# A conditional block of attention-free layers on one core: the hand-over tables of the second half in another order of the same steps

## The chip, the cores and the metric

The kernel runs on one core of one Trainium2 chip. Five engines work side by side, each through its own instructions in program order: TensorE (PE; its weight loads are listed as PEld), VectorE (DVE), ScalarE (ACT), GpSimd (POOL) and SyncE (SP), which only issues transfers. They wait for one another through semaphores. The metric is the device time of one execution in microseconds (us), as the median over several runs.

## What is computed

The input is 32 batches of 128 tokens of 512 numbers. The block has two halves. The first changes masked tokens only, the second all of them:

```
m = mask[:, :, None]
shift, scale, gate_msa = split(silu(t) @ ada_w + ada_b, 3)
norm = where(m, layernorm(x) * (1 + scale) + shift, 0)
ssm_out = where(m, fwd(norm) + bwd(norm), 0)        # two MLPs of 512 x 512 x 512, gelu
x = x + gate_msa * ssm_out
shift_mlp, scale_mlp, gate_mlp = split(silu(t) @ ffada_w + ffada_b, 3)
ff_norm = layernorm(x) * (1 + scale_mlp) + shift_mlp
h = gelu(ff_norm @ ff_w1 + ff_b1)                   # 512 -> 1024
return x + gate_mlp * (h @ ff_w2 + ff_b2)           # 1024 -> 512
```

All of it is float32.

## The kernel before

**The first half.** The masked tokens are packed into slots, 128 to a tile, and only these pass through the first half. Its results are written to rows in DRAM (`x1_rows`).

**The second half** does the feed-forward part for the 32 batches in four pairs p = 0 to 3 of two sides with four batches each. A side's x is loaded by SyncE (`load_side`; the steps X0 and X1 load the sides of pair p + 2 at the end of pair p). Then `take_first_half` (L904) writes the first half's results over the masked rows: per tile of 128 tokens one indirect transfer on GpSimd's queue, called a gather here. The steps x20 to x27 are the eight gathers for pair 2; a step name that begins with "n" belongs to the next pair (nx20 stands in the table of pair 0 and x26 and x27 in that of pair 1). A gather needs its tile's load to have landed. VectorE then takes the statistics of each tile (steps b00 to b13, L937 and L938; v0, v1 at L942; r0, r1 on GpSimd at L945), and the tile is normalised (n..), turned (z..), moved across partitions by SyncE (m...) and scaled by ScalarE (c..., L968).

**Both matrix products are done by a fast scheme with seven products per 2 x 2 split, on two levels.** In the first product (`FirstProduct`) the outer products are the streams 1, 2, 5, 6, 3, 7, 4, and each has seven inner groups P1 to P7, of four matmuls each (L1155). So 6P3 is a group on PE, the third inner product of stream 6. Around the groups of a stream j stand its sums: jc5 (ScalarE, a copy out of PSUM), js (VectorE L1175, seeds one bank from the other), jw12 and jw22 (GpSimd L1182), jk11 and others (ScalarE L1197), je (VectorE L1188), jj22 and jj21 (VectorE L1207), ja.. (GpSimd L1216). All VectorE sums among these read a PSUM bank (`a_m` in the rows). Stream sums of tokens (steps tj0 to tj3, lines 1091, 1095, 1098 and 1101 for j = 1 to 4; blocks A1 to A4 at L1021) read and write SBUF alone. Those of pair p + 1 are named nt10 to nt43 in the table of pair p.

In the second product (`SecondProduct`) a group is PnU0 and the like (L1387, up to eight matmuls), F.., B., T., U. are VectorE sums (F02 at L1294), and three of its products are split again (`Inner`): 5i3, 6i4, 7i4 and so on are groups of eight small matmuls on PE (L1473), S1i4 to S4i4 their sums on GpSimd (L1462), C5i4 copies on ScalarE (L1500), V6i4 and V7i4 sums on VectorE (L1505), J40 a sum on VectorE (L1420). The result is multiplied by the gate and added to x: K... on ScalarE (L1343), G... on GpSimd (L1349) or VectorE (L1331), R... (L1356, L1338), and stored by SyncE (o.., L1369).

**What sets the order.** Each of these steps is put into a table by name, and `ORDER[p]` is a text of names. The steps are run in the order of the text, so each engine's program is the text's order as far as its own steps go:

```
class Steps:
    def put(self, name, f, *args):
        assert name not in self.todo, name
        self.todo[name] = lambda: f(*args)

    def run(self, order):
        for name in order or list(self.todo):
            self.todo.pop(name)()
        assert not self.todo, list(self.todo)
...
        steps.run(ORDER.get(p, "").split())
```

No scheduler stands behind it: what an engine's queue holds at its head, it waits for, and everything behind waits with it. The table of pair p runs from stream 6 of that pair (6P1 is its first name in pair 0) to stream 2 of the next pair (n2P4 is near its end). The gather is this:

```
    def take_first_half(p, xs, which=range(2 * G)):
        for i in which:
            b = 2 * p * G + i
            nc.gpsimd.indirect_dma_start(
                out=xs[i // G][i % G // 2][:, i % 2],
                ...
```

At the end of pair p six gathers of pair p + 2's tiles stand on GpSimd, and behind them the first GpSimd sum of the next pair's stream 6, 6w12, which 6e on VectorE and then 6P3 on PE wait for.

## Time and profile before

| what | value |
|---|---|
| three runs of the kernel before | 451.76, 452.56, 452.85 us; median 452.56 |
| the profiled execution | 454.02 us, its span 452.3 us |
| granted TensorE clock, mean | 0.994 |
| busy in the span | PE 436.5, DVE 336.8, POOL 263.9, ACT 204.8 us |
| moved by DMA | 70.89 MB, mean 157 GB/s |
| the reordered part of the span | from 99.11 us to the end |

A row of the trace in time shows start, duration, engine, line, operation, the names of output and inputs, shape, and in brackets how long the engine sat idle before it and what released it. "x4" says that four instructions which follow one another are joined in one row. TensorE's ends are modelled, so its rows overlap by some tenths of a microsecond, and the spacing of starts tells more. All numbers are microseconds from the start of the span. The profile describes one execution, so its span and its own time belong together, and the median of the runs is a little lower.

### The profile page before, as it was taken

What the parts mean: (1) busy time and instruction counts of PE and PEld (TensorE: products, weight loads), DVE (VectorE), ACT (ScalarE), POOL (GpSimd) and SP (SyncE); (2) the same over time, 40 slices, a digit from 0 to 9 for tenths busy, and PEclk for the clock granted to TensorE, in tenths of its full rate; (3) what the DMA queues carried; (4) which work ended last, traced back from release to release, by engine and by line L of the source; (5) the groups of instructions that cost most, each with busy time, mean ns of one, the idle gap of its engine ahead of it and who ended that gap; (6) DMA issues with size and microseconds to landing.
All of it is one profiled execution on the core that took longest, in us unless ns stands there. A gap on an engine that the chain in (4) does not pass through costs nothing.

```text
span 452.3 us, 7030 instructions
## 1 busy us (share of the span) xinstructions
PE 436.5 (97%) x2435; PEld 372.1 (82%) x2435; DVE 336.8 (74%) x592; ACT 204.8 (45%) x453; POOL 263.9 (58%) x226
## 2 busy tenths in 40 slices
PE   8999989999999999989999989999999999999992
PEld 4884675688888998878889978888899988888992
DVE  5788788878996689969762799898727994454265
ACT  3133127254582773534856635438756244553120
POOL 4211460089942894998618666896187616922991
PEclk9999999999999999999999999999999999999997
DMA  7999449894155507851375068614750354113005
GB/s 252 367 395 410 168 89 326 274 349 137 36 145 94 135 1 243 279 159 43 95 139 140 2 223 269 188 40 77 154 145 1 144 205 124 39 57 131 0 5 186
DMA packets 57044, 70.89 MB, mean 157 GB/s; under 512 B 34740, under 2 KB 36108, under 8 KB 55982
## 3 DMA queue, kind: packets, MB, share of 16 engines
q1 hardware_dynamic: 51742, 67.72, 47.7%
q0 software_dynamic: 3008, 2.15, 1.7%
q10 hardware_dynamic: 2256, 0.54, 0.7%
q8 instruction: 21, 0.34, 0.3%
q14 instruction: 17, 0.14, 0.1%
HBM read 56.71 MB, written 13.70 MB: 156 GB/s over the span
## 4 chain that ended last, share of the span: by engine, by line
PE 72%; DMA 11%; DVE 6%; POOL 5%; issue 5%; ACT 0%; POOLq 0%; SPq 0%; DVEq 0%; ACTq 0%
PE a_m L1155 17%; PE e_m L1155 13%; PE e_o L1387 12%; PE a_o L1387 11%; PE one_P L1473 6%; DMA fw<-in_L_cond_ff_w_dram 3%; PE po_s L222 3%; DMA w<-in_L_cond_bwd_w_dram 3%; PE a_o L1473 3%; PE five_P L1473 2%; PE e_o L1473 2%; DMA x_wide<-t_s 2%; POOL x L904 2%; POOL t L1349 1%; DMA x<-in_x_dram 1%
## 5 line engine op out<-in xcount | busy, mean ns | idle before, releaser
L1349 POOL TENSOR_TENSOR t<-t,gate 128x512 f32<-128x512 f32 x16 | 24.0, 1507 | 62.5 <-ACT t L1343 62.5
L1182 POOL TENSOR_TENSOR ha<-p_m,ha 128x512 f32<-128x512 f32 x20 | 25.5, 1274 | 48.2 <-ACT ha L1197 36.8
L968 ACT ACTIVATE xT<-xT,modT 128x128 f32<-128x128 f32 x112 | 46.4, 485 | 4.7 <-DMA xT<-xn 3.3
L904 POOL DMA_INDIRECT x<-x_rows,slot_i x24 | 31.5, 1311 | 8.2 <-issue 6.6
L1207 DVE TENSOR_TENSOR hb<-a_m,hb 128x512 f32<-128x512 f32 x40 | 27.2, 679 | 10.0 <-PE a_m L1155 7.3
L1197 ACT COPY ha<-e_m 128x512 f32<-128x512 f32 x32 | 18.6, 586 | 35.0 <-PE e_m L1155 29.2
L1125 ACT ACTIVATE hb<-hb,biasT 128x256 f32<-128x256 f32 x64 | 28.2, 500 | 13.0 <-DVE hb L1207 13.0
L1387 PE MATMUL a_o<-t,s 128*128 128x256 f32 x128 | 29.6, 379 | 0.0
L1387 PE MATMUL a_o<-fw,ha 128*128 128x256 f32 x128 | 29.4, 379 | 0.0
L1387 PE MATMUL e_o<-fw,s 128*128 128x256 f32 x128 | 29.2, 380 | 0.1
L1125 ACT ACTIVATE ha<-e_m,biasT 128x256 f32<-128x256 f32 x48 | 20.1, 469 | 19.9 <-PE e_m L1155 19.9
L1387 PE MATMUL e_o<-fw,ha 128*128 128x256 f32 x128 | 28.4, 379 | 0.0
L222 PE MATMUL po_s<-w,h_s 128*128 128x512 f32 x64 | 28.4, 594 | 0.0
L1387 PEld LDWEIGHTS e_o<-fw,s 128*128 128x128 f32 x128 | 24.2, 190 | 3.8 <-DVE s L1294 0.5
L1182 POOL TENSOR_TENSOR hb<-p_m,hb 128x512 f32<-128x512 f32 x20 | 26.3, 1319 | 1.4 <-DVE hb L1207 1.0
L1387 PEld LDWEIGHTS a_o<-fw,ha 128*128 128x128 f32 x128 | 24.3, 190 | 3.3
L1387 PEld LDWEIGHTS e_o<-fw,ha 128*128 128x128 f32 x128 | 24.3, 190 | 3.3
L1387 PEld LDWEIGHTS a_o<-t,s 128*128 128x128 f32 x128 | 23.7, 190 | 2.9
L1398 DVE TENSOR_TENSOR e_o<-a_o,p_o 128x512 f32<-128x512 f32 x16 | 11.1, 693 | 18.1 <-PE a_o L1387 17.1
L1155 PE MATMUL a_m<-xT,tw 128*128 128x256 f32 x96 | 24.3, 379 | 0.0
L1169 ACT COPY p_m<-e_m 128x512 f32<-128x512 f32 x27 | 15.7, 585 | 17.6 <-PE e_m L1155 17.6
L1155 PE MATMUL e_m<-s,fw 128*128 128x256 f32 x92 | 23.7, 381 | 0.0
(280 smaller groups left out, 1150.8 us busy)
## 6 DMA issues: line engine op xcount, KB each, us to landing
x<-in_x_dram SPq DMA_DIRECT2D x16, 512.0 KB, 7.1
tw<-t_rows SPq DMA_DIRECT2D x16, 512.0 KB, 3.6
gate<-gate_rows SPq DMA_DIRECT2D x8, 1024.0 KB
out_dram<-x SPq DMA_DIRECT2D x15, 512.0 KB, 4.2
xT<-xn SPq DMA_DIRECT2D x104, 64.0 KB, 2.2
tw<-t_rows SPq DMA_DIRECT2D x16, 384.0 KB
ada_f<-in_L_cond_ffada_w_dram SPq DMA_DIRECT2D x4, 768.0 KB, 14.7
ada_a<-in_L_cond_ada_w_dram SPq DMA_DIRECT2D x4, 512.0 KB, 3.5
```

The source lines that it names most:

```text
L222: nc.tensor.matmul(po, h[f][:, ts(i, P)], w[:, f, :], start=(f == 0 and seeded is None), stop=(f == HC - 1), skip_group_check=seeded is no ...
L904: nc.gpsimd.indirect_dma_start(out=xs[i // G][i % G // 2][:, i % 2], out_offset=None, in_=x1_rows, in_offset=bass.IndirectOffsetOnAxis(ap= ...
L968: nc.scalar.activation(out, src, AF.Identity, bias=shift, scale=scale)
L1125: nc.scalar.activation(dst[:, n], src[:, n], AF.Gelu_apprx_tanh, bias=biasT[:, f : f + 1])
L1155: nc.tensor.matmul(bank[:, ts(n, QT)].rearrange("p (i b c) -> p i b c", i=2, c=R), self.w_block(j, product)[:, ts(n, P)], self.x_block(j, ...
L1169: nc.scalar.copy(self.p5[j], self.fives[j].rearrange("p (n s) -> p n s", n=2))
L1182: nc.gpsimd.tensor_tensor(self.place(RESULT[j], c), self.p5[j], other, ALU.add)
L1197: nc.scalar.copy(self.place(RESULT[j], c), src)
L1207: nc.vector.tensor_tensor(dst, a, other, ALU.add)
L1349: nc.gpsimd.tensor_tensor(view, view, self.gate[side][:, 2 * c : 2 * c + 2, part], ALU.mult)
L1387: nc.tensor.matmul(bank[:, ts(i, D // 2)], src[:, k, ts(i, P)], w[:, k, :], start=False, stop=True, skip_group_check=True,)
L1473: nc.tensor.matmul(out[:, i % out.shape[1]], src[:, k, ts(i, P)], w[:, k, :], start=(start and (i == 0 or out.shape[1] == 1) and k == 0), ...
```

## The change

The texts of `ORDER` for all four pairs (lines 1695 to 1774) are replaced. No step is added or removed, no line elsewhere differs, and the engines execute as many instructions as before. A line or two of the table of pair 0, around the end, shows the kind of the difference:

```
-            nt20 o01 nt30 o10 n1P4 nt12 X0 n5P1 n5s nt33 n2P3 n2k12 nx20 n2P7 n1k21 n5P2 nt32 n5P6
+            n2k11 n2w12 n2e nt32 n2w22 nx20 n5c5 nt22 n5P1 n5s n2P7 nt20 nx21 n2P3 nx23 n5P2 nt13
```

What happens to the places that matter here is read from the engines' programs.

**The end of pair 0 on VectorE.** From the sum n2e (the row of `e_m_2`) on. L1091 to L1101 are token sums of pair 1, `hb<-a_m_2` at L1207 is n2j22 the first time and n2j21 the second, and `e_m_5` at L1188 is n5e. Before:

```order
L1188 TENSOR_TENSOR e_m_2_1570<-a_m_2_1571,ha_1564 128x512
L1095 TENSOR_TENSOR xn_sy_1607<-sx_1442,s_1_1443 128x512
L1098 TENSOR_TENSOR s_1_1443<-s_1_1443 128x2x256
L1091 TENSOR_TENSOR sx_1442<-xT_1_1280 128x512
L1098 TENSOR_TENSOR s_1_1444<-s_1_1444 128x256
L1098 TENSOR_TENSOR xT_1_1280<-xT_1_1280 128x2x256
L1207 TENSOR_TENSOR hb_1565<-a_m_2_1571,hb_1565 128x2x256
L1101 TENSOR_TENSOR s_1_1443<-s_1_1443,xn_sy_1607 128x2x256
L1095 TENSOR_TENSOR xn_sy_1607<-sx_1442,xT_1_1280 128x512
L1095 TENSOR_TENSOR xn_sy_1607<-sx_1442,xT_0_1234 128x512
L1101 TENSOR_TENSOR s_1_1444<-s_1_1444,xn_sy_1607 128x256
L1207 TENSOR_TENSOR hb_1565<-a_m_2_1571,hb_1565 128x2x256
```

Now:

```order
L1188 TENSOR_TENSOR e_m_2_1572<-a_m_2_1573,ha_1569 128x512
L1098 TENSOR_TENSOR xT_1_1298<-xT_1_1298 128x2x256
L1095 TENSOR_TENSOR xn_sy_1632<-sx_1464,xT_1_1298 128x512
L1095 TENSOR_TENSOR xn_sy_1632<-sx_1464,s_1_1465 128x512
L1091 TENSOR_TENSOR sx_1464<-s_1_1466 128x256
L1207 TENSOR_TENSOR hb_1570<-a_m_2_1573,hb_1570 128x2x256
L1095 TENSOR_TENSOR xn_sy_1632<-sx_1464,xT_0_1203 128x512
L1101 TENSOR_TENSOR xT_1_1298<-xT_1_1298,xn_sy_1632 128x2x256
L1101 TENSOR_TENSOR xT_0_1203<-xT_0_1203,xn_sy_1632 128x2x256
L1098 TENSOR_TENSOR s_1_1465<-s_1_1465 128x2x256
L1188 TENSOR_TENSOR e_m_5_1615<-a_m_5_1616,p_m_5_1630 128x512
L1207 TENSOR_TENSOR hb_1570<-a_m_2_1573,hb_1570 128x2x256
```

Five token sums (one of them 256 wide) stood between n2e and n2j22; now four do (one 256 wide). Four more led to n2j21; now four lead to n5e, and n2j21 follows it at once.

**The inner products of pair 1 on GpSimd.** `si_1_P` and `hb` at L1462 are the sums S1i4 to S4i4 (the last one, `hb<-hb,si_1_P`, is S4i4, which 7i4 reads), and L1349 are gate products (G001 of the tile `t_001`, G101 of `t_101`). Before:

```order
L1462 TENSOR_TENSOR si_1_P_2116<-hb_1565 128x512
L1349 TENSOR_TENSOR t_100_2005<-t_100_2005,gate_0_1906 128x512
L1462 TENSOR_TENSOR si_1_P_2163<-si_1_P_2116,hb_1565 128x512
L1462 TENSOR_TENSOR hb_1565<-hb_1565 128x2x256
L1349 TENSOR_TENSOR t_101_2175<-t_101_2175,gate_0_1906 128x512
L1349 TENSOR_TENSOR t_001_2113<-t_001_2113,gate_0_1906 128x512
L1462 TENSOR_TENSOR hb_1565<-hb_1565,si_1_P_2163 128x2x256
```

Now:

```order
L1462 TENSOR_TENSOR si_1_P_2136<-hb_1570 128x512
L1462 TENSOR_TENSOR si_1_P_2138<-si_1_P_2136,hb_1570 128x512
L1349 TENSOR_TENSOR t_001_2120<-t_001_2120,gate_0_1867 128x512
L1462 TENSOR_TENSOR hb_1570<-hb_1570 128x2x256
L1462 TENSOR_TENSOR hb_1570<-hb_1570,si_1_P_2138 128x2x256
L1349 TENSOR_TENSOR t_101_2164<-t_101_2164,gate_0_1867 128x512
```

Two gate products stood directly ahead of S4i4, and now one stands ahead of S3i4 and the other behind S4i4.

**The end of pair 1 on VectorE**, with the same steps of the next pair; `e_m_2` at L1188 is n2e again. Before:

```order
L1188 TENSOR_TENSOR e_m_2_2219<-a_m_2_2220,ha_2229 128x512
L1095 TENSOR_TENSOR xn_sy_2255<-sx_2157,s_2_2134 128x256
L1095 TENSOR_TENSOR xn_sy_2255<-sx_2157,s_2_2133 128x512
L1098 TENSOR_TENSOR xT_0_1860<-xT_0_1860 128x2x256
L1098 TENSOR_TENSOR xT_1_1943<-xT_1_1943 128x2x256
L1098 TENSOR_TENSOR s_2_2133<-s_2_2133 128x2x256
L1207 TENSOR_TENSOR hb_2230<-a_m_2_2220,hb_2230 128x2x256
L1095 TENSOR_TENSOR xn_sy_2255<-sx_2157,xT_0_1860 128x512
L1098 TENSOR_TENSOR s_2_2134<-s_2_2134 128x256
L1101 TENSOR_TENSOR s_2_2133<-s_2_2133,xn_sy_2255 128x2x256
L1101 TENSOR_TENSOR s_2_2134<-s_2_2134,xn_sy_2255 128x256
L1207 TENSOR_TENSOR hb_2230<-a_m_2_2220,hb_2230 128x2x256
```

Now:

```order
L1188 TENSOR_TENSOR e_m_2_2228<-a_m_2_2229,ha_2234 128x512
L1098 TENSOR_TENSOR s_2_2177<-s_2_2177 128x2x256
L1091 TENSOR_TENSOR sx_2237<-s_2_2178 128x256
L1098 TENSOR_TENSOR xT_1_1943<-xT_1_1943 128x2x256
L1095 TENSOR_TENSOR xn_sy_2256<-sx_2237,s_2_2178 128x256
L1098 TENSOR_TENSOR s_2_2178<-s_2_2178 128x256
L1207 TENSOR_TENSOR hb_2235<-a_m_2_2229,hb_2235 128x2x256
L1095 TENSOR_TENSOR xn_sy_2256<-sx_2237,xT_0_1888 128x512
L1098 TENSOR_TENSOR xT_0_1888<-xT_0_1888 128x2x256
L1101 TENSOR_TENSOR s_2_2177<-s_2_2177,xn_sy_2256 128x2x256
L1188 TENSOR_TENSOR e_m_5_2246<-a_m_5_2247,p_m_5_2266 128x512
L1101 TENSOR_TENSOR s_2_2178<-s_2_2178,xn_sy_2256 128x256
```

n2j22 is the seventh row in both; ahead of it stood one narrow token sum (256 wide) and four wide ones, and now three narrow and two wide stand there; three token sums further on comes n5e, where four led to n2j21 and n5e stood behind the last row shown.

Other places are told in words. On PE the groups of pair 0 read 6i4, 4i7, n1P5, n1P1, 2i4, 7i4 where 6i4, n1P5, 7i4 stood; in pair 1 they read 6i4, n1P5, 7i4, n1P1 where 6i4, n1P5, n1P1, 7i4 stood. In pair 2 the VectorE sum F02 stands ahead of the statistics b11, b12 and b13, where it stood behind them and v1. In pair 1 the statistics b12 stand ahead of 4s and behind x26 and x27, where they stood behind 3j21.

142 lines of the change are left out of this document (71 added, 71 removed).

## The prediction

> **What bounds the kernel now.** I first read the page's table of busy time. It names the engine that is never idle for long:
>
> ```profile
> PE 436.5 (97%) x2435; PEld 372.1 (82%) x2435; DVE 336.8 (74%) x592; ACT 204.8 (45%) x453; POOL 263.9 (58%) x226
> ```
>
> TensorE (PE) is busy for 436.5 of the span's 452.3 us. The change removes no matmul, so all it can gain is PE's idle time, 15.8 us. The second view is the table by stage; its columns are start:end, length, then busy time of PE, PEld, DVE, ACT and POOL, the granted clock, the DMA share and GB/s:
>
> ```profile
> 0.00:99.11 99.11, 95.93 (x540) 64.91 (x541) 78.08 (x190) 33.39 (x72) 32.49 (x51) 1.00 0.84 295
> 99.11:168.00 68.89, 68.89 (x383) 62.35 (x382) 58.19 (x93) 40.20 (x91) 50.13 (x39) 1.00 0.40 98
> 312.00:443.30 131.30, 131.30 (x772) 120.06 (x770) 78.63 (x114) 59.87 (x135) 77.69 (x61) 1.00 0.32 95
> 443.30:452.30 9.00, 0.27 (x3) 0.08 (x1) 3.44 (x8) 0.00 (x0) 0.00 (x0) 0.71 0.52 179
> ```
>
> The reordered part runs from 99.11 on. Up to there PE is idle for 3.18 us, and nothing the change moves lies there. The last row is the tail behind the last matmuls: 8.73 us idle, and the last steps stand as they did. That leaves 15.8 − 3.2 − 8.7 = 3.9 us of idle, none of it in the 200 us of the second and third row. The third view, PE's own rows in time (start, duration of the group, matmuls, what it waited for), shows the four places where it lies:
>
> ```profile
> 168.72 1.13 PE L1155 MATMUL e_m<-s,fw 128*128 128x256 f32 x4
> 170.24 1.16 PE L1473 MATMUL one_P<-fw,hb 128*128 128x128 f32 x8 [0.40 <-DVE xn_d L1505]
> ...
> 195.50 1.03 PE L1155 MATMUL a_m<-sx,tw 128*128 128x256 f32 x4
> 198.45 1.13 PE L1155 MATMUL e_m<-xn_sy,tw 128*128 128x256 f32 x4 [1.92 <-DVE e_m L1188]
> 199.42 1.03 PE L1155 MATMUL a_m<-xn_sy,tw 128*128 128x256 f32 x4
> ...
> 261.24 1.03 PE L1155 MATMUL a_m<-xT,fw 128*128 128x256 f32 x4
> 263.72 1.13 PE L1473 MATMUL one_P<-fw,hb 128*128 128x128 f32 x8 [1.46 <-POOL hb L1462]
> ...
> 308.81 2.26 PE L1387 MATMUL e_o<-fw,s 128*128 128x256 f32 x8
> 310.91 1.03 PE L1155 MATMUL a_m<-xT,tw 128*128 128x256 f32 x4
> 311.77 1.03 PE L1155 MATMUL e_m<-s,tw 128*128 128x256 f32 x4
> ```
>
> I measure a loss from start to start, since the ends are modelled. A group of four takes 311.77 − 310.91 = 0.86, one of eight 1.72, and a group that had to wait costs 0.1 more itself (198.45 to 199.42 is 0.97). So the losses are A, at 168.72: 1.52 − 0.86 + 0.1 = 0.76. B, at 195.50: 2.95 − 0.86 + 0.1 = 2.19. C, at 261.24: 2.48 − 0.86 + 0.1 = 1.72. D, at 308.81: 2.10 − 1.72 = 0.38. Together 5.05 us (more than the 3.9 of idle, since a group's modelled end, 1.03 behind its start, reaches past the 0.86): the most that any order of these steps can win.
>
> **Why B is late.** B is the group 6P3 of pair 1, and it waits for a VectorE sum (6e), which waits for the GpSimd sum 6w12, which stands behind six gathers. GpSimd's rows (start, duration), the first three of the gathers, two of the others, and 6w12:
>
> ```profile
> 183.93 3.50 POOL L904 DMA_INDIRECT x<-x_rows,slot_i  x1 [0.28 <-POOL hb L1182]
> 187.73 2.35 POOL L904 DMA_INDIRECT x<-x_rows,slot_i  x1 [0.30 <-issue]
> 190.38 2.08 POOL L904 DMA_INDIRECT x<-x_rows,slot_i  x1 [0.30 <-issue]
> 192.77 0.99 POOL L904 DMA_INDIRECT x<-x_rows,slot_i  x1 [0.30 <-issue]
> 195.37 1.00 POOL L904 DMA_INDIRECT x<-x_rows,slot_i  x1 [0.30 <-issue]
> 196.39 1.27 POOL L1182 TENSOR_TENSOR ha<-p_m,ha 128x512 f32<-128x512 f32 x1
> ```
>
> From 6w12's start to PE's is 198.45 − 196.39 = 2.06. A gather takes 1.00 and 0.30 to the next, but three took 3.50, 2.35 and 2.08. VectorE beside them:
>
> ```profile
> 185.76 0.69 DVE L1098 TENSOR_TENSOR xT<-xT 128x512 f32<-128x512 f32 x1
> 186.36 0.69 DVE L1207 TENSOR_TENSOR hb<-a_m,hb 128x512 f32<-128x512 f32 x1
> 189.10 0.69 DVE L1207 TENSOR_TENSOR hb<-a_m,hb 128x512 f32<-128x512 f32 x1
> 191.50 0.70 DVE L1175 TENSOR_TENSOR e_m<-a_m,ha 128x512 f32<-128x512 f32 x1
> ```
>
> The first gather ends at 187.43, 1.07 after the sum of L1207 starts; the second at 190.08, 0.98 after the next; the third at 192.46, 0.96 after L1175. These three read a PSUM bank (a_m). What fills the time between them, without a gap, are token sums of lines 1091 to 1101, both of whose inputs lie in SBUF, each 0.60 behind the last (186.36 − 185.76; 0.34 where it is 256 wide). I take from this: a gather that stands before an unbroken row of such sums is served when the row is broken by a sum that reads PSUM, and ends about 1.05 after. The next boundary supports it and tempers it:
>
> ```profile
> 276.66 2.39 POOL L904 DMA_INDIRECT x<-x_rows,slot_i  x1 [1.39 <-DMA x<-in_x_dram]
> 279.35 1.15 POOL L904 DMA_INDIRECT x<-x_rows,slot_i  x1 [0.30 <-issue]
> 286.13 1.28 POOL L1182 TENSOR_TENSOR ha<-p_m,ha 128x512 f32<-128x512 f32 x1
> ...
> 278.00 0.69 DVE L1207 TENSOR_TENSOR hb<-a_m,hb 128x512 f32<-128x512 f32 x1
> ```
>
> The gather of 2.39 ends 1.05 after the L1207 sum at 278.00; the one at 279.35 passed between two token sums. Here 6w12 came at 286.13 and PE lost nothing: 6P3 ran in its slot (288.95), 0.76 after 286.13 + 2.06.
>
> **The change, part by part.** Nothing is added or removed; four orders are replaced. Every step has the same instructions, its DMAs included, so what moves is what waits for what.
>
> *A.* 7i4 waited for the VectorE step V6i4. In the new order 4i7, two first groups of the next pair and 2i4 stand between 6i4 and 7i4, over 3 us of PE work: the wait is gone. +0.76.
>
> *C.* 7i4 of pair 1 waited for the GpSimd step S4i4 (L1462), which stood behind two gate products:
>
> ```profile
> 258.88 3.56 POOL L1349 TENSOR_TENSOR t<-t,gate 128x512 f32<-128x512 f32 x2 [4.06 <-ACT t L1343]
> 262.40 1.26 POOL L1462 TENSOR_TENSOR hb<-hb,si_P 128x512 f32<-128x512 f32 x1
> ...
> 253.36 2.54 DVE L1021 TENSOR_TENSOR s<-xT 128x1024 f32<-128x1024 f32 x1
> ```
>
> GpSimd had idled 4.06 for ScalarE's K011 before. Now one product stands ahead of S3i4 and S4i4 and the one that needs K011 behind them, which frees 4.06 + 1.78; 7i4 itself stands one group, 0.86, earlier. What is late next is VectorE: V6i4 now stands directly behind A1 (L1021) and a few 0.6 us sums. A1 has lasted 2.54 (the row at 253.36) where others last 1.2; with 1.2 the cover holds, with 2.54 some 0.3 is lost. I take half, 0.15: +1.57.
>
> *D.* P5U0 of pair 2 waited for F02:
>
> ```profile
> 309.20 0.68 DVE L1294 TENSOR_TENSOR s<-hb 128x512 f32<-128x512 f32 x1
> ```
>
> It stood behind two tiles' statistics; it now stands ahead of them. They are 1.6 of VectorE work and the wait was 0.38: gone. +0.38.
>
> *B.* The order of both engines at the end of pair 0 is new. Let R be the slot in which 6P3 would start without loss; 6w12 has to start by R − 2.06. PE reaches n2P6, which releases n2e, 18 groups ahead: R − 15.5; with the product's own time and the sum's wait n2e starts at R − 13.8. It and three wide token sums and a narrow one (4 × 0.60 + 0.34) lie ahead of n2j22, a PSUM sum: R − 11.0. That and four wide ones lie ahead of n5e (R − 8.0), n5e itself, n2j21, two wide and two narrow ones ahead of 6s (R − 5.2). The first gather is ready at about R − 13: it writes rows into a tile that the load X0 fills, which follows a store, and before it landed at 183.15, 13.2 ahead of the slot 195.50 + 0.86 = 196.36:
>
> ```profile
> 177.09 6.06 DMA x<-in_x_dram
> ```
>
> So by the rule the first ends 1.05 after n2j22 (R − 10.0), the second after n5e (R − 7.0; n2j21 begins too early for the third), the third after 6s (R − 4.1), and the last three at 1.30 each: R − 0.2. 6w12 starts there and 6P3 at R + 1.9. Loss 1.9 for 2.19: +0.29. From below, gathers that all pass between sums as the one at 279.35 did make it 0; from above, with the first opening missed for a later X0, one gather more is left at 1.30: 3.2. I keep 1.9, the value that the three openings before B gave.
>
> *E, new.* At the end of pair 1 n2j22 now comes after two wide and three narrow token sums, and n5e three wide ones later. Counted in the same way from n2P6, 17 groups ahead: n2j22 at R − 10.5, n5e at R − 8.1, and n2j21, which waits for its product, lets the third through; the others end at R − 9.4, − 7.0, − 5.7, − 3.7, − 2.4 and − 1.1. 6w12 starts at R − 1.1, 6P3 at R + 1.0: lost 1.0, where before nothing was. From below 0, from above 2.3 (one opening missed, 1.30 more): −1.0.
>
> The sum: 0.76 + 1.57 + 0.38 + 0.29 − 1.0 = 2.0 us. The profiled execution took 454.02, 1.7 more than its span; less 2.0 it is 452.0. The median of the three runs shown is 452.56, so 2.0 less there is 450.6. All losses gone: 452.56 − 5.05 = 447.5. B at 3.2, E at 2.3 and the waits A, C and D replaced by others of 1.5 in all: 7.0 lost for 5.05, 454.5.
>
> **The rivals.** *First: a gather waits for one sum at most.* Then it costs 1.00 and half a sum, 0.35; six with their 0.30 are 9.6, from R − 13 to R − 3.4, ahead of R − 2.06 at both ends of a pair, and B and E are 0: 5.05 − 0.15 = 4.9 gained, 447.7. The gather at 279.35 (1.15) speaks for it. The one of 3.50 speaks against it: several sums started and ended inside it. [...]
>
> *Second: the new orders miss the openings.* B costs 3.2 and E 2.3 while A, C and D are won: 5.05 − 5.5 − 0.15 = 0.6 lost, 453.2. For it: both places rest on a load that lands after a store, and the trace shows one gather already waiting 1.39 for that load.
>
> *Third: VectorE stands behind a landing.* Its queue is in program order, and b12, the statistics of a gathered tile, now stands ahead of 4s in pair 1, with x26, its gather, shortly before; before, it stood behind 3j21:
>
> ```profile
> 209.42 1.01 POOL L904 DMA_INDIRECT x<-x_rows,slot_i  x1 [0.30 <-issue]
> 213.60 0.68 DVE L937 BATCH_NORM_STATS2 st<-x 128x6 f32<-128x512 f32 x1
> ...
> DMA to landing us min/median/max: 2.6/3.8/7.6
> ```
>
> Behind b12 wait 4s and 3j21, and PE's 4P2 waits for 4s. Between x26 and 4P2 lie some six groups, 5.4; a landing of 2.7, b12's 0.7 and 4s's 0.7 leave 1.3. From a landing of 4.0 on it costs; at the longest, 7.6, 3.6: 450.6 + 3.6 = 454.2, slower. For it: half of the landings are over 3.8. Against it: the long ones are counted with the time in which the gather itself was held, and none of those is held at this place, where no token sums run.
>
> **How the numbers follow.** The forecast's case, 450.6, has 0.50: its rule explains four gathers of five, its sizes are counted. The first rival has 0.24, for the one gather that slipped. The second has 0.15, the third 0.11. A measurement here tells 0.3% (1.36 us) from no change. The forecast's case lies 0.6 inside that border (451.2); I give two thirds of it, 0.34, to faster, 0.14 to the same and 0.02 to slower. With the first rival's 0.24 and 0.01 of the second, faster has 0.59; the second's other 0.14 brings the same to 0.28; the third brings slower to 0.13. The range from 447.5 to 453.9 takes in the first two rivals and leaves out the third. The forecast's case alone, with B between 0.6 and 3.2 and E between 0 and 2.3, has 448.3 to 453.2.
>
> **What would show it.** In the changed profile, PE shows no wait between 6i4 and 7i4 in pair 0, at most 0.3 in pair 1, and none before P5U0; 6w12 of pairs 1 and 2 still starts directly behind the sixth gather, and the two first gathers of each last over 2 us and end about 1.05 after n2j22 and n5e. I am wrong if those gathers take 1.0 to 1.7 (then the first rival), if PE's rows show a wait behind b12 (the third), or if PE's idle from 99.11 to the tail differs from 3 us by over 1.5.

## The result, and the profile after

The changed kernel took 448.23 us (median of four runs, 447.90 to 449.09), the kernel before beside it 452.50 (four runs, 451.76 to 452.85). The ratio is 0.9911 with a 95% interval of 0.9892 to 0.9930: 4.27 us faster, where 2.0 had been forecast. The time lies in the stated range, and the sign is the one that was given the most chance, but more than half of the gain was not in the sum.

The page's table of busy time and the first line of the chain that ended last, of the changed kernel:

```profile
PE 435.6 (98%) x2435; PEld 372.8 (84%) x2435; DVE 328.0 (73%) x592; ACT 205.5 (46%) x453; POOL 260.5 (58%) x226
...
PE 95%; DVE 2%; POOL 1%; issue 0%; ACT 0%; DVEq 0%
```

The chain runs almost wholly over PE. VectorE is busy for 8.8 us less than in the kernel before (336.8) with the same 592 instructions, and GpSimd for 3.4 less (263.9). Waiting inside an instruction counts as busy (A1, a sum below, is listed with 2.54 in the one kernel and 1.21 in the other), so I take this for waiting that went.

The two profiled executions can't be subtracted as they are, since 6.0 us lie between their spans (452.3 and 446.3) and 4.27 between the medians. I compare PE from the first matmul group of the reordered part to the last group instead. Of the kernel before, those two rows:

```profile
99.11 1.03 PE L1155 MATMUL a_m<-xn_sy,tw 128*128 128x256 f32 x4
...
442.52 1.06 PE L1473 MATMUL last<-fw,hb 128*128 128x128 f32 x8
```

And of the changed kernel:

```profile
97.41 1.03 PE L1155 MATMUL a_m<-xn_sy,tw 128*128 128x256 f32 x4
...
436.40 1.06 PE L1473 MATMUL last<-fw,hb 128*128 128x128 f32 x8
```

442.52 − 99.11 = 343.41 became 436.40 − 97.41 = 338.99: 4.42 us, which agrees with the medians' 4.27. The other 1.70 of the start (99.11 − 97.41) arose where nothing was changed. The tail is as it was: 452.3 − 442.52 = 9.8 and 446.3 − 436.40 = 9.9.

What is left of PE's losses in the changed kernel, as rows in time. The first two rows lie in pair 0, the others are the place that was called B:

```profile
152.75 1.06 PE L1473 MATMUL five_P<-t,si_P 128*128 128x128 f32 x8
153.84 0.82 PE L1473 MATMUL one_P<-fw,ha 128*128 128x128 f32 x5
...
193.31 1.03 PE L1155 MATMUL a_m<-sx,tw 128*128 128x256 f32 x4
194.39 1.13 PE L1155 MATMUL e_m<-xn_sy,tw 128*128 128x256 f32 x4
```

Counted from start to start as in the prediction: 153.84 − 152.75 is 1.09 where the rows around it are 0.89 apart, so 0.20 is lost there, and that is new. At B, 194.39 − 193.31 − 0.86 + 0.1 = 0.32 is lost, where it was 2.19. At A, C, D and E nothing is: E's place, 6P3 of pair 2, is the second of these two rows, 0.86 behind the first:

```profile
282.37 1.03 PE L1155 MATMUL a_m<-sx,tw 128*128 128x256 f32 x4
283.23 1.03 PE L1155 MATMUL e_m<-xn_sy,tw 128*128 128x256 f32 x4
```

So 5.05 of losses became 0.52, a gain of 4.5 for the 4.4 measured on PE.

**The gathers** are where the forecast and the trace part. GpSimd's rows at the end of pair 0 and at the end of pair 1 of the changed kernel: the first of the six gathers, and 6w12 behind the sixth:

```profile
181.35 1.44 POOL L904 DMA_INDIRECT x<-x_rows,slot_i  x1 [0.16 <-POOL hb L1182]
183.09 1.14 POOL L904 DMA_INDIRECT x<-x_rows,slot_i  x1 [0.30 <-issue]
184.53 2.70 POOL L904 DMA_INDIRECT x<-x_rows,slot_i  x1 [0.30 <-issue]
187.54 2.16 POOL L904 DMA_INDIRECT x<-x_rows,slot_i  x1 [0.30 <-issue]
...
192.31 1.29 POOL L1182 TENSOR_TENSOR ha<-p_m,ha 128x512 f32<-128x512 f32 x1
...
271.69 1.47 POOL L904 DMA_INDIRECT x<-x_rows,slot_i  x1 [1.10 <-DMA x<-in_x_dram]
273.47 1.48 POOL L904 DMA_INDIRECT x<-x_rows,slot_i  x1 [0.31 <-issue]
...
280.20 1.28 POOL L1182 TENSOR_TENSOR ha<-p_m,ha 128x512 f32<-128x512 f32 x1
```

The first gather took 1.44 where it had taken 3.50. VectorE beside it, from the sum n2e on:

```profile
180.53 0.69 DVE L1188 TENSOR_TENSOR e_m<-a_m,ha 128x512 f32<-128x512 f32 x1
181.12 0.68 DVE L1098 TENSOR_TENSOR xT<-xT 128x512 f32<-128x512 f32 x1
181.72 0.69 DVE L1095 TENSOR_TENSOR xn_sy<-sx,xT 128x512 f32<-128x512 f32 x1
...
183.26 0.69 DVE L1207 TENSOR_TENSOR hb<-a_m,hb 128x512 f32<-128x512 f32 x1
```

The gather ended at 182.79, before the PSUM sum n2j22 (183.26) had begun: it was let through between two token sums. By the rule of the prediction that cannot happen.

### The profile page after: what moved, and what is told of

It is laid out like the page before. It is cut to its first block, busy times and chain, and to the rows that moved or that the text cites. A ratio compares the mean times of both kernels' runs of the same rounds, so it can differ in the third digit from the quotient of the medians.

```text
span 446.3 us, 7040 instructions
## 1 busy us (share of the span) xinstructions
PE 435.6 (98%) x2435; PEld 372.8 (84%) x2435; DVE 328.0 (73%) x592; ACT 205.5 (46%) x453; POOL 260.5 (58%) x226
## 4 chain that ended last, share of the span: by engine, by line
PE 95%; DVE 2%; POOL 1%; issue 0%; ACT 0%; DVEq 0%
PE a_m L1155 20%; PE e_m L1155 16%; PE a_o L1387 12%; PE e_o L1387 12%; PE one_P L1473 7%; PE po_s L222 6%; PE ph_s L205 5%; PE a_o L1473 4%; PE e_o L1473 2%; PE five_P L1473 2%; PE ph_s L681 2%; PE a_m_alone L1155 1%; PE pm_ss L308 1%; PE pm_f L308 1%; PE part_s L342 0%; PE pl_s L255 0%
## 5 line engine op out<-in xcount | busy, mean ns | idle before, releaser
L1349 POOL TENSOR_TENSOR t<-t,gate 128x512 f32<-128x512 f32 x16 | 23.1, 1444 | 61.4 <-ACT t L1343 57.3
L1207 DVE TENSOR_TENSOR hb<-a_m,hb 128x512 f32<-128x512 f32 x40 | 27.4, 686 | 15.7 <-PE a_m L1155 12.1
L904 POOL DMA_INDIRECT x<-x_rows,slot_i x24 | 29.3, 1219 | 7.4 <-issue 5.7
L1188 DVE TENSOR_TENSOR e_m<-a_m,ha 128x512 f32<-128x512 f32 x20 | 13.9, 696 | 14.5 <-PE a_m L1155 5.1
```

Source lines behind the costliest of these rows:

```text
L904: nc.gpsimd.indirect_dma_start(out=xs[i // G][i % G // 2][:, i % 2], out_offset=None, in_=x1_rows, in_offset=bass.IndirectOffsetOnAxis(ap= ...
L1207: nc.vector.tensor_tensor(dst, a, other, ALU.add)
L1349: nc.gpsimd.tensor_tensor(view, view, self.gate[side][:, 2 * c : 2 * c + 2, part], ALU.mult)
```

## The experiments

All times are medians beside runs of the kernel before on the same chip, and the ratios carry 95% intervals. Single runs of one kernel spread by up to 1.4%, and the medians of the kernel before lie between 451.74 and 453.11, so ratios are compared and not times from different chips. Losses on PE are counted from start to start, each in the one profiled execution. The five kernels with rows of sums appended were executed once each, and only their rows are read. Of an order or of code, only the stretch that matters is shown.

### Which table brings it

The first two put one table of the change into the kernel before. `t0_only` takes the whole new text of pair 0, `t1_only` that of pair 1 alone.

> The kernel before with the table of pair 0 alone from the changed kernel; pairs 1 to 3 as before. Theory S (a gather that stands beside token sums can also be let through between two of them, by chance, and always by a sum that reads PSUM): A (0.76) and B (2.0) are gone, C and D stay, so about 2.7 us less than before, 449.8 us; the six gathers at the end of pair 0 take less than 11.5 us from the start of the first to the end of the last. Theory P, the one of the prediction (only a sum that reads PSUM lets a gather through): A 0.76 and 0.3 of B are won, 451.5 us, and the six gathers take 12 us or more. Theory Q (a gather waits for one sum at most): the gathers are never longer than 1.8 us, B is 0, 449.6 us.

Measured: 450.61 us (9 runs) beside 452.94 (20), ratio 0.9955 (0.9934 to 0.9976). The six gathers repeat those of the changed kernel to 0.01 us: 1.43, 1.15, 2.69, 2.16, 1.00, 0.99. They are no accident of one execution. A and B are gone. The mixture of old and new tables has a wait of its own (1.41 on PE, ahead of the group at 189.59). D remains. And C is gone too, although the table of pair 1 is that of the kernel before. The reason stands in its rows of VectorE and GpSimd, A1 first:

```profile
251.37 1.29 DVE L1021 TENSOR_TENSOR s<-xT 128x1024 f32<-128x1024 f32 x1
...
251.54 2.25 POOL L1462 TENSOR_TENSOR hb<-hb 128x512 f32<-128x512 f32 x1
```

A1 took 1.29 instead of 2.54, and the GpSimd sum S3i4 took 2.25. In the kernel before A1 had the 2.54 of the row at 253.36, and S3i4 this:

```profile
253.52 1.30 POOL L1462 TENSOR_TENSOR hb<-hb 128x512 f32<-128x512 f32 x1
```

Both times A1's row begins 0.16 to 0.17 ahead of S3i4's (253.36 and 253.52, 251.37 and 251.54). In the one S3i4 passes and A1 waits, in the other A1 passes and S3i4 waits. What makes the difference is not shown.

> The kernel before with the table of pair 1 alone from the changed kernel. Theory S and theory Q: C (1.72) is won, nothing is lost at the end of pair 1, 450.8 us. Theory P: C is won but 1.0 us is lost at the end of pair 1, 451.8 us. In either B stays at about 2 us, since the gathers at the end of pair 0 stand as before; if B moved too, the table of pair 1 would have a hand in it, which none of the three says.

Measured: 451.52 us (12 runs) beside 452.94 (20), ratio 0.9972 (0.9956 to 0.9987). The gathers at the end of pair 0 are those of the kernel before (3.62, 2.34, 2.09, 1.00, 1.00, 1.00), those at the end of pair 1 those of the changed one (1.49, 1.48, 1.00 and so on). Each order of steps brings its own holds along, whatever stands around it. A and D remain, B shows as 0.51 and 1.52 at two groups, C and E are 0.

### What the held gathers cost

`no_gathers` leaves out the six gathers of pair 2's tiles at the end of pair 0, so these tiles go without the results of the first half.

```
         for i in which:
+            if p == 2 and i < 6:
+                continue
             b = 2 * p * G + i
```

> The kernel before without the six gathers at the end of pair 0 (first-half results of six tiles of pair 2 are left out, so these rows hold x itself). If the gathers are what makes 6w12 late (all three theories), B goes and nothing else does: 2.1 to 2.2 us less, 450.3 us, and PE shows no wait before 6P3 of pair 1. If 6w12 waits for something else as well (its copy on ScalarE, the third sum), part of B stays: over 451 us.

Measured: 450.42 us (6 runs) beside 452.94, ratio 0.9936 (0.9914 to 0.9957). B is 0 on PE, the other losses stand. So B is wholly due to these gathers, and its price, 2.2 of 2.5 us, is what the prediction had.

### What a gather waits for

`gather_alone` appends six rows behind the changed kernel: in each, VectorE runs some 30 sums and GpSimd is given six gathers at the row's beginning. The rows differ in what the sums read and where they write.

```
+    for kind in ("apart", "chained", "narrow", "strided", "psum", "mixed"):
+        for i in range(6):
+            nc.vector.tensor_tensor(mg[i][:, :8], mt[4][:, 0, :8], mt[5][:, 0, :8], ALU.add)
+        part(kind, 0)
+        for i in range(6):
+            nc.gpsimd.indirect_dma_start(
+                out=mg[i],
...
+        for n in range(1, 48 if kind == "narrow" else 30):
+            part(kind, n)
```

> The changed kernel, and behind its last store six rows of 30 (48) VectorE sums each, with six gathers of the kind of L904 beside each row: sums of separate tiles in SBUF, sums each of which reads the result of the one before, sums 256 wide, sums of tiles in two strips, sums with one operand in PSUM, and rows in which each fifth sum reads PSUM. Theory S: beside rows without PSUM the gathers are spread, some 1.0 to 1.7, some 2 to 4 us; with PSUM all are 1.0 to 1.2 us; with each fifth, up to 4 us. Theory P: beside rows without PSUM no gather ends before the row does (up to 17 us); with each fifth they end 1.05 after such a sum starts. Theory Q: 1.0 to 1.8 us in every row.

Measured, GpSimd's rows: the first gather of the first row (sums of two SBUF tiles), one of the second (the same sums in place), the first of the row that reads PSUM, and the first of the row in which every fifth sum reads PSUM:

```profile
449.28 19.14 POOL L2030 DMA_INDIRECT mg<-x_rows,slot_i  x1 [0.48 <-DVE mg L2027]
...
479.36 1.50 POOL L2030 DMA_INDIRECT mg<-x_rows,slot_i  x1 [0.31 <-issue]
...
539.44 1.00 POOL L2030 DMA_INDIRECT mg<-x_rows,slot_i  x1 [10.91 <-DVE mg L2027]
...
557.84 3.39 POOL L2030 DMA_INDIRECT mg<-x_rows,slot_i  x1 [10.89 <-DVE mg L2027]
```

All the cases occur here. Beside sums that read PSUM a gather takes its 1.00. In a row of two-SBUF sums it is either held until the row is over (19.14, and 17.08 in the row of narrow sums) or let through at once (1.22 to 1.51). In the broken row all six are served at the PSUM sums (3.39, then 2.70 or 2.71 each), as the prediction's rule says. So the rule describes a gather that is held, and is silent on whether it is held.

Two kernels then took the openings themselves. `j21_later` moves the PSUM sum n2j21 of the changed kernel two token sums back:

```
-  nt41 nt30 n5e n2j21 nt23 nx25 nt40 nx24 nt33 nt43
+  nt41 nt30 n5e nt23 nx25 nt40 n2j21 nx24 nt33 nt43
```

> The changed kernel with one VectorE sum moved: n2j21, which reads PSUM, two token sums later (behind nt40), so that it stands where the fourth gather of pair 0's end (nx22, 2.16 us) waits. Theory O (a sum that reads PSUM always lets a gather through): that gather ends about 1.0 behind the new place of n2j21 (1.3 us in all), 0.8 us sooner, the 0.22 at B goes, and the time is 0.2 us less, within the measurement's reach of no change. Theory R (it is chance): its time may be anything from 1.0 to 2.7 us.

Measured: 449.19 us (6 runs) beside 453.11 (17), ratio 0.9913 (0.9888 to 0.9937). The fourth gather took 1.23 instead of 2.16, and B's last 0.2 is gone on PE. That is too small to see in the time: the ratio is the changed kernel's.

`no_openings` goes on and moves all three PSUM sums behind the row, which is then twelve token sums without a break:

```
-  nt13 n2j22 nx22 n1k21 ... nt30 n5e n2j21 nt23 nx25 nt40 nx24 nt33 nt43 ng1121
+  nt13 nx22 n1k21 ... nt30 nt23 nx25 nt40 nx24 nt33 nt43 n2j22 n5e n2j21 ng1121
```

> The changed kernel with n2j22, n5e and n2j21 of pair 0's end moved behind nt43, so that all eleven token sums stand in an unbroken row and no sum that reads PSUM lies between them. Theory P (only sums that read PSUM let a gather through): the gathers that meet the row end behind it, at n2j22; the first takes about 5 us, and 6P3 loses 3 us or more: 451 us. Theory S (some boundaries between token sums let one through, and which ones is fixed by the sums): the first is let through where nt22 follows nt32, as in the changed kernel (1.4 us), at least one more within the row, and 6P3 loses 1 to 2.5 us: 449.5 to 450.5 us.

Measured: 449.14 us (4 runs) beside 453.11, ratio 0.9904 (0.9877 to 0.9932). The first two gathers; the others took 1.49, 1.24, 1.00 and 1.00:

```profile
182.80 1.43 POOL L904 DMA_INDIRECT x<-x_rows,slot_i  x1 [0.17 <-POOL hb L1182]
184.53 1.15 POOL L904 DMA_INDIRECT x<-x_rows,slot_i  x1 [0.30 <-issue]
```

With no opening at all the gathers were faster than with three (the six together 7.31 instead of 9.43). B loses nothing, but the delayed sum n5e costs another group of PE, at 190.20, 0.6. By the prediction's rule the first would have lasted until the row's end, over 6 us. The rule is refuted for this place.

### What decides between held and let through

`which_sums` asks whether it is the operation or the form: ten rows of 23 sums, of nine kinds (add, subtract, in place, narrow, two pieces, one tile twice and so on; the tenth row repeats the first), with three gathers behind the third sum.

```
+    for of_row in (
+        add_apart, sub_apart, add_two, sub_two, add_place, sub_place, sub_half, add_high, add_same, add_apart
+    ):
...
```

> The changed kernel and behind it ten rows of 23 VectorE sums with three gathers each, which begin behind the third sum. The rows differ in one thing each: addition or subtraction, operands in one strip or two, a separate result or one in place, 256 wide, other tiles, one tile as both operands, and the first row once more at the end. In the earlier run rows of additions with separate results let no gather through, and rows of subtractions (in place, or in two strips) let each through at the first boundary. If the operation or the form of the operands decides, the rows fall into the two kinds by it (one kind about 12 us for the first gather, the other 1.0 to 1.6 us each). If the moment of arrival decides, rows of one form differ, and the first and the last row too.

Measured: the first gather was held to the row's end in all ten (12.79 to 12.89 us, 7.46 in the row 256 wide); in the first row:

```profile
453.98 12.89 POOL L2018 DMA_INDIRECT mg<-x_rows,slot_i  x1 [2.52 <-DVE mg L2014]
```

Forms that had let gathers through in `gather_alone` held them here. The form of the sums does not decide.

`who_begins` asks whether it is who starts first: 27 rows of 16 sums, with a gather, or in the last eleven a GpSimd sum of two SBUF tiles, started ahead of the row by 0 to 20 sums of 8 numbers.

```
+    for kind, delays in (("gather", range(0, 16)), ("sum", range(0, 22, 2))):
...
+            for k in range(delay):
+                small(ms[:, 8 * (k % 8) : 8 * (k % 8) + 8])
+            for n in range(16):
+                nc.vector.tensor_tensor(mt[0][:, n % KC], mt[1][:, n % KC], mt[2][:, n % KC], ALU.add)
...
```

> The changed kernel and behind it 27 rows of 16 VectorE sums with two SBUF operands, all of one form. In the first 16 a gather starts on GpSimd, and the row begins 0 to 15 small sums that read PSUM (each 0.08 us) later; in the last 11 a GpSimd sum of 1.27 us starts in the gather's place and the row 0 to 20 small sums later. Two more gathers follow on GpSimd in each. [...] Theory M (the moment of arrival within a sum decides, whatever went before): gathers of both kinds occur in one row, and which one goes with their distance from the last boundary. Theory K (chance): no order in it.

Measured: the sixteen rows with gathers alternate, let through and held, whatever the head start. The first gathers of the rows with 0 and 1 small sums (those with 2 and 3 took 1.35 and 10.45; from the eighth row on it is the second gather that is held, 9.44 to 10.03, and the first takes its 1.00, with the longer head start: at 534.03 in the eighth):

```profile
449.02 1.22 POOL L2010 DMA_INDIRECT mg<-x_rows,slot_i  x1 [0.16 <-issue]
...
457.58 10.31 POOL L2010 DMA_INDIRECT mg<-x_rows,slot_i  x1 [3.83 <-DVE ms L2007]
```

The rows with GpSimd sums: let through, held (10.81), and then nine times let through (1.26). From the third of these rows on, the first gather behind the GpSimd sum was let in too, 1.28 to 1.45; the sum and that gather of the fourth:

```profile
686.85 1.26 POOL L2026 TENSOR_TENSOR mg<-mt,mt 128x512 f32<-128x512 f32 x1 [6.66 <-DVE mg L2007]
688.26 1.29 POOL L2010 DMA_INDIRECT mg<-x_rows,slot_i  x1
```

For the rows with gathers the head start does not decide whether one is held, only which one. But the alternation points to what precedes the row: behind a held row VectorE has to wait for the late gathers, and so stands idle ahead of the next (2.52 behind the first row of `gather_alone`); behind a row that let its gathers through it runs straight on (behind the second row there, with no idle time at 494.94). VectorE's idle time alone it is not, by my estimate: eight of those nine rows come 11.14 to 11.17 behind the row ahead, of which the GpSimd sum's 1.26 and sixteen sums at 0.60 leave 0.3. There a GpSimd sum was at work, or in the last row just done, when the row began (4 to 20 small sums, 0.08 each in `after_a_break`, after the sum's start). From the third of these rows on the gather behind the sum was let in (1.28 to 1.45). The rows with gathers alternate, so a gather at work there did not do the same.

`idle_before` asks for that: sixteen rows of 14 sums with two gathers each, all behind twelve PSUM sums, half of them with VectorE idle for some 2 us as well (GpSimd waits some 16.3 ahead of these and 14.14 ahead of the others), half with one small sum more.

```
+        for k in range(12):
+            nc.vector.tensor_tensor(ma, mp, mt[1][:, 1], ALU.add)
+        if idle:
+            for k in range(3):
+                nc.scalar.copy(ma, ma)
...
```

> The changed kernel and behind it 16 rows of 14 VectorE sums with two SBUF operands, all of one form, each with two gathers that start at the row's beginning, and each behind 12 sums that read PSUM, in which GpSimd has time to finish. Before 8 of the rows VectorE waits about 2 us for ScalarE, before the other 8 it runs on without a break; in half of each there is one small sum more ahead of the row. In the run before, rows behind a wait of VectorE let the gathers through (1.0 to 1.6 us) and rows that followed without a break held one to their end (over 8 us). Theory D (a break of VectorE ahead of the row decides): the 8 rows with the wait let them through, the other 8 hold one. Theory N (the number of instructions ahead decides): the rows go by the small sum. Theory T (it goes by turns): held and let through alternate with the rows, whatever is ahead. Theory M (the moment of the gather's start within the first sum decides): the rows go by the distance from the row's first sum to the gather's start.

Measured: all 32 gathers were let through (1.32 to 1.51), idle or not; the first of a row without idle time:

```profile
488.60 1.49 POOL L2011 DMA_INDIRECT mg<-x_rows,slot_i  x1 [14.14 <-DVE mg L2008]
```

Neither the idle time nor the small sum makes a difference, and what the theories of this run expected did not come. What all rows share is a long stretch of PSUM sums ahead of them.

`after_a_break` therefore varies that stretch: 26 rows, each behind twelve two-SBUF sums and a break of 0 to 8 PSUM sums, with the gather asked for 0 to 6 sums into the row.

```
+    for number, (broken, ahead, wide) in enumerate(
+        [(m, 0, 512) for m in (0, 1, 2, 3, 4, 5, 6, 8)] * 2
+        + [(m, 3, 512) for m in (1, 3, 6)]
+        + [(6, 1, 512), (6, 2, 512), (6, 6, 512)]
+        + [(m, 0, 256) for m in (1, 2, 3, 6)]
...
```

> The changed kernel and behind it 26 rows of VectorE sums with two SBUF operands, with one gather each. Ahead of each row stand 12 sums of the same kind beside which no gather runs, and then a break of 0 to 8 sums that read PSUM (0.60 us each); the gather starts in the first sum behind the break in 16 rows (each break twice), behind 3, 1, 2 or 6 sums in six rows, and beside sums 256 wide in four. [...] Theory T (it goes by turns) or K (chance): the two halves differ. Theory O (a sum that reads PSUM ahead of the row is enough): let through from a break of 1 on.

Measured, the gathers of the rows with breaks of one sum and of two:

```profile
470.55 7.82 POOL L2027 DMA_INDIRECT mg<-x_rows,slot_i  x1 [11.42 <-DVE mg L2026]
490.61 1.20 POOL L2027 DMA_INDIRECT mg<-x_rows,slot_i  x1 [12.24 <-DVE mg L2026]
```

No break gave 7.91, breaks of 3, 4, 5, 6 and 8 sums 1.20 or 1.21, and the second time round all eight came out as the first time. With the gather three sums into the row: held behind a break of one sum (7.83), let through behind three and six (1.20). Behind a break of six: let through one and two sums into the row, held six sums into it (7.83). In rows 256 wide: held behind one (7.98), let through behind two, three and six (1.00). This is the clean result of the study. A row that follows two-SBUF sums at no or one PSUM sum's distance holds the gather until it is broken (7.82 to 7.98); from two sums on, a gather that is asked for in the first sums of the row gets in at the first boundary (1.00 to 1.21). So the border lies between one sum and the small one, 0.60 and 0.08 or some 0.7 us, and two and the small one, 1.4 (488.87 to 490.26). One PSUM sum is not enough, and since both halves agree, neither turns nor chance explain it.

### The break in the kernel itself

In the kernel before, two PSUM sums directly precede the row at the end of pair 0, 1.19 us; in the changed one there are four, 2.4 us (178.73 to 181.12). Of the kernel before, the first of the two PSUM sums and the first token sum behind them:

```profile
182.43 0.69 DVE L1338 TENSOR_TENSOR x<-a_o,x 128x512 f32<-128x512 f32 x1
...
183.62 0.68 DVE L1095 TENSOR_TENSOR xn_sy<-sx,s 128x512 f32<-128x512 f32 x1
```

`longer_break` moves one step of the kernel before, the token sum nt23, from its place between those PSUM sums to behind n2e. That leaves four PSUM sums ahead of the row (2.57 us), and lengthens the row.

```
-            4i4 n1P3 o00 n1P7 nt13 n5c5 G101 n1k12 n1j22 nt23 n2P2 n2k11 n2w12 n2w22 R101 n2P6 n2e
-            nt20 o01 nt30 o10 n1P4 nt12 X0 n5P1
+            4i4 n1P3 o00 n1P7 nt13 n5c5 G101 n1k12 n1j22 n2P2 n2k11 n2w12 n2w22 R101 n2P6 n2e
+            nt23 nt20 o01 nt30 o10 n1P4 nt12 X0 n5P1
```

> The kernel before with one VectorE sum moved: at the end of pair 0 the token sum nt23 stands behind n2e, not two sums ahead of it. So four sums that read PSUM (2.4 us) follow one another ahead of the row of token sums in which the first gather starts, where two did (1.2 us). [...] If the break ahead does not matter here, the first gather stays over 3 us and B at 2.1, 452.5 us.

Measured: 449.97 us (12 runs) beside 452.70 (18), ratio 0.9949 (0.9923 to 0.9976). Its first and fifth gather; those between took 1.14, 1.49 and 1.23:

```profile
183.03 1.54 POOL L904 DMA_INDIRECT x<-x_rows,slot_i  x1 [0.39 <-POOL hb L1182]
...
191.64 1.00 POOL L904 DMA_INDIRECT x<-x_rows,slot_i  x1 [2.30 <-DMA x<-in_x_dram]
```

One step, moved to where by the prediction's rule it makes things worse, lets the gathers through. They then run ahead of the second side's load, and the fifth waits 2.30 for it, so B keeps 0.65 of its 2.19. C is gone here as in `t0_only` (A1 1.30, S3i4 2.25), and A and D remain.

`shorter_break` does the reverse to the changed kernel: the token sum nt32 goes from behind n2e to ahead of the last two PSUM sums, which leaves 1.20 us of break.

```
-  nW2 R101 R111 n5P5 n1P4 n2k11 n2w12 n2e nt32 n2w22
+  nW2 R101 nt32 R111 n5P5 n1P4 n2k11 n2w12 n2e n2w22
```

> The changed kernel with one VectorE sum moved: at the end of pair 0 the token sum nt32 stands ahead of the last two sums that read PSUM (R111 and n2e), not behind them, so that the break ahead of the row is 1.2 us and not 2.4. [...] If the break does not matter, the first gather stays at 1.4 us and B at 0.2: 448.3 us.

Measured: 449.09 us (7 runs) beside 452.70, ratio 0.9932 (0.9907 to 0.9957). The gathers were not held: 1.47, and 1.00 to 1.09, and B is 0. So the length of the break alone does not decide. The break here and in the kernel before are the same to 0.01 us (1.20 and 1.19), between the two lengths of `after_a_break`, and they went one each way. One row differs beside them: the GpSimd sum 2w22 directly ahead of the gathers took 1.84,

```profile
181.16 1.84 POOL L1182 TENSOR_TENSOR hb<-p_m,hb 128x512 f32<-128x512 f32 x1
```

where it takes 1.27 in `t0_only`, `j21_later` and `no_openings`. It started together with nt32 (181.16 and 181.18), lost 0.57, about a sum's length, and was let in just ahead of the gathers. That a GpSimd instruction which has just been let in eases the next one's way is only a guess. The nine rows of `who_begins` with a GpSimd sum ahead fit it; no run tests it in the kernel.

### What C was

By the prediction, 7i4 of pair 1 was late for the GpSimd sum S4i4 behind two gate products. These are the steps G010 and G011 (they work on the tiles `t_001` and `t_101`, and were called G001 and G101 ahead of the prediction). `c_products_later` moves the two behind S4i4 in the kernel before:

```
-  G110 S3i4 c033 n1c5 n1P1 E21 V6i4 G011 J40 G010 n1s 7i4 G111 c022 C7i4 R110 S4i4 c030
+  G110 S3i4 c033 n1c5 n1P1 E21 V6i4 J40 n1s 7i4 G111 c022 C7i4 R110 S4i4 G011 G010 c030
```

> The kernel before with one change: in pair 1 the two gate products on GpSimd that wait for K011 (G011 and G010) are run behind S4i4, not ahead of it. Theory H (7i4 of pair 1 is late because S4i4 stands behind the products, which wait for K011): C goes, 1.6 to 1.7 us less than before, 451.2 us; A, B and D stay at 0.67, 2.1 and 0.37. [...]

Measured: 455.41 us (12 runs) beside 453.11 (17), ratio 1.0041 (1.0011 to 1.0071): 0.4% slower. S4i4 was done at 258.89, 4.8 earlier than before (263.66), and yet 7i4 waited longer, 2.70. The row of V6i4 on VectorE, then that of 7i4 on PE:

```profile
263.50 0.41 DVE L1505 TENSOR_TENSOR xn_d<-one_P,xn_d 128x256 f32<-128x256 f32 x1
...
264.07 1.13 PE L1473 MATMUL one_P<-fw,hb 128*128 128x128 f32 x8 [2.54 <-DVE xn_d L1505]
```

7i4 waits for V6i4 on VectorE, as at A. It adds to the bank that V6i4 reads, and it stands ahead of S4i4 in the table, so it can't wait for S4i4. Nor does it read S4i4's result, as was said ahead of the prediction: in the program 7i4 reads what S3i4 writes, and S4i4 writes for 3i4. In the kernel before the two happened to end together: S4i4 at 263.66, and V6i4, whose row is

```profile
263.16 0.41 DVE L1505 TENSOR_TENSOR xn_d<-one_P,xn_d 128x256 f32<-128x256 f32 x1
```

at 263.57. The trace named the later one as releaser. V6i4 was late because VectorE, on which it stood behind A1, A3, A2, nt10 and five shorter sums, ran late: A1 had taken 2.54, and nt10, a token sum that takes 0.69 elsewhere, 1.64. With the products moved, A1 took 2.56 and nt10 1.65 as before, and A2 2.29: VectorE lost time beside other GpSimd instructions as well.

`c_both_parts` moves the products and V6i4. V6i4 got ahead of 6i4, whose product it adds, so that product is left out of the sum.

```
-  1i4 nt10 3i7 S2i4 C1i4 E20 4i7 6i4 K011 n1P5 G110 S3i4 c033 n1c5 n1P1 E21 V6i4 G011 J40
+  1i4 V6i4 nt10 3i7 S2i4 C1i4 E20 4i7 6i4 K011 n1P5 G110 S3i4 c033 n1c5 n1P1 E21 J40
```

> The kernel before with two changes at C: in pair 1 the gate products G011 and G010 are run behind S4i4 on GpSimd, as in the run before, and on VectorE V6i4 is run ahead of the token sum nt10 and of E20, G110 and E21. Theory W (7i4 of pair 1 waits for two chains that are late together, S4i4 on GpSimd and V6i4 on VectorE, and only both moves free it): C falls from 1.62 (and 2.70 with the products alone) to under 0.4; A 0.67, B 2.1 and D 0.37 stay, and the time is about 1.4 us below the kernel before, 451.1 us. If a third chain is late, C keeps over 1 us.

Measured: 453.13 us (12 runs) beside 451.74 (17), ratio 1.0026 (0.9992 to 1.0060), unclear. 6i4 now waited 2.12 for the copy C1i4, which stood behind V6i4, so this run tells nothing of C. It showed something else, which stands under the hardware below.

`c_both_again` puts V6i4 directly behind 6i4, and nt10 behind V6i4, with the products moved as well:

```
-  1i4 nt10 3i7 S2i4 C1i4 E20 4i7 6i4 K011 n1P5 G110 S3i4 c033 n1c5 n1P1 E21 V6i4 G011 J40
+  1i4 3i7 S2i4 C1i4 E20 4i7 6i4 V6i4 nt10 K011 n1P5 G110 S3i4 c033 n1c5 n1P1 E21 J40
```

> The kernel before with G011 and G010 behind S4i4 on GpSimd, and on VectorE V6i4 directly behind E20 and the token sum nt10 behind V6i4 (in the run before this one V6i4 was put ahead of 6i4, whose product it adds, so that product was left out of the sum, and C1i4 and 6i4 waited for V6i4: it could say nothing of C). Theory W (7i4 of pair 1 waits for two chains that are late together, S4i4 on GpSimd and V6i4 on VectorE): C falls from 1.62 (2.70 with the products alone) to under 0.4 and nothing else moves: 1.3 to 1.7 us below the kernel before. If a third chain is late, C keeps over 1 us.

Measured: 452.89 us (12 runs) beside 452.72 (17), ratio 1.0010 (0.9988 to 1.0033). 7i4 ran in its slot, and the next group, 2i4, waited for the following VectorE sum instead. PE's row, and VectorE's A2 ahead of it, A1 having taken 2.54 once more:

```profile
263.74 2.05 PE L1473 MATMUL a_o<-t,hb 128*128 128x128 f32 x16 [1.10 <-DVE a_o L1420]
...
257.90 2.30 DVE L1021 TENSOR_TENSOR s<-s,xT 128x1024 f32<-128x1024 f32 x1
```

VectorE is behind by A1's and A2's waits, 1.3 and 1.1, and moving one sum forward only hands the wait to the next. With the old table of pair 1, C is gone where A1 took 1.3 and nt10 0.69 (`t0_only`, `longer_break`). With the new one (`t1_only` and the changed kernel) it is gone as well, and there A2, A3 and nt10 stand behind V6i4.

## Why the prediction was right or wrong

**What bounds the kernel, and where it loses: right.** The four places and their prices were the right ones. The changed kernel won 4.4 of the 5.05 that they were said to hold.

**A and D: right.** 0.76 and 0.38, both gone as the order alone said.

**B and E: wrong, and this is the step that failed**: "a gather that stands before an unbroken row of such sums is served when the row is broken by a sum that reads PSUM". The places of VectorE's sums were counted rightly. With the slot of 6P3 at R = 193.31 + 0.86 = 194.17, n2j22 came at R − 10.9 (said: R − 11.0) and n5e at R − 7.9 (said: R − 8.0), n5e's row being

```profile
186.26 0.70 DVE L1188 TENSOR_TENSOR e_m<-a_m,p_m 128x512 f32<-128x512 f32 x1
```

But the first gather did not wait for n2j22. B lost 0.32 where 1.9 was forecast, and E nothing where 1.0 was: 1.6 + 1.0 = 2.6 us. Less the new 0.20 in pair 0, and with the 0.15 that C did not lose, that is the 2.5 between 2.0 forecast and the 4.5 counted on PE. The rule was drawn from three gathers of one boundary, and the one gather that contradicted it, of 1.15, was called a tempering. It is the rule of a gather that is held. Whether one is held is another question, and `gather_alone`, `no_openings` and `longer_break` show that it was the one that mattered.

**C: the price right, the first cause wrong.** 7i4 never waited for S4i4. It waited for V6i4, and moving the gate products away cures nothing (`c_products_later`). What the prediction put second, that V6i4 "now stands directly behind A1 (L1021) and a few 0.6 us sums", is what cures C in the changed kernel: between A1 and V6i4 only two sums are left of eight. Its A1, 6i4, V6i4 and 7i4 are

```profile
253.37 1.21 DVE L1021 TENSOR_TENSOR s<-xT 128x1024 f32<-128x1024 f32 x1
...
255.40 1.06 PE L1473 MATMUL one_P<-t,si_P 128*128 128x128 f32 x8
...
256.50 0.42 DVE L1505 TENSOR_TENSOR xn_d<-one_P,xn_d 128x256 f32<-128x256 f32 x1
...
257.16 1.05 PE L1473 MATMUL one_P<-t,hb 128*128 128x128 f32 x8
```

V6i4 starts 0.04 behind the end of 6i4, whose product it adds, and ends 0.24 ahead of 7i4; VectorE had waited 0.48 for PE in between. Had A1 taken 2.54, VectorE's spacing of 1.13 + 1.33 for A1 and 0.60 for each of the two sums would have put V6i4 at 257.03, and 7i4, 0.15 behind its end as in the kernel before, at about 257.6. My estimate of the loss is then 0.4, near the 0.3 that the prediction named. That the gain at C came out is in part luck all the same: the main reason given for it was not the reason.

**The rivals.** The first, that a gather waits for one sum at most, gave 447.7 and came nearest. As a mechanism it is wrong too: 2.70 and 2.16 in the changed kernel and 19.14 in `gather_alone` are more than one sum. That its time came nearest is therefore in part luck. The second, missed openings, fell with the rule. The third did not show: PE has no wait behind b12.

**What is shown and what is open.** Shown: gathers beside a row of two-SBUF sums are either held until the row breaks (7.46 to 19.14 beside rows without a break) or let in at the first boundary (1.0 to 1.6), each order repeats its own pattern, the form of the sums does not decide, nor the head start in rows with gathers, and a break of two PSUM sums and a small one (1.4 us) ahead of the row decides in `after_a_break` (1.20, against 7.82 behind one PSUM sum). Putting the longer break into the kernel before let its gathers through (1.54 for the first, where it had taken 3.50). Open is the exact rule. Breaks of 1.2 us went both ways; in `gather_alone` the first row held its gather although VectorE had stood idle for 6.74 ahead of it, with six small sums of two SBUF tiles (0.5) in between; and the small sums of `who_begins`, up to eighteen ahead of a row with gathers (1.3 us), did not act as a break. Beside that, a GpSimd sum at work when the row begins may let the next gather in (1.28 to 1.45 in `who_begins`). A1 and S3i4 change places at a distance of 0.16 to 0.18 in both outcomes, so it is not the distance. What it is, no run shows.

No version clearly beats the changed kernel: `j21_later` at 0.9913 and `no_openings` at 0.9904 lie within its interval.

## What to carry to other kernels

A row of VectorE sums that read two SBUF tiles can hold GpSimd's gathers off for its whole length (19.14 beside thirty sums in `gather_alone`), so put three or more sums that read PSUM directly ahead of such a row (behind breaks of three to eight the gathers of `after_a_break` took 1.20 or 1.21; two of them, 1.2 us, went either way in this kernel), ask for the gathers at its beginning (six sums into the row one was held, 7.83), and read in the trace whether they were let in. Take the releaser that a trace names as a guess until the program says that the one can wait for the other: an instruction that ended 0.1 us earlier may be the true one (V6i4 at 263.57, S4i4 at 263.66). When a wait is removed by moving one instruction of a queue that is late as a whole, the next instruction takes it over (2i4 with 1.10 in `c_both_again`).
